# Moving an addition to the stop behind the row of maxima, and a small softmax away from a turn's boundary, in a two-layer cross-attention kernel

## The chip, the core and the metric

One core of one Trainium2 chip runs the whole program. The metric is device time in microseconds (us). The kernel before takes 3610.84 us, the median of three runs (3610.59 to 3620.91). A profiled execution of it took 3614.53 us. Everything is float32.

Five engines work side by side: PE (TensorE, matrix products; its weight loads are listed as PEld), DVE (VectorE), ACT (ScalarE), POOL (GpSimd) and SP (SyncE, which here issues the DMAs). Each takes its own instructions in its own order and waits on semaphores for the others.

## What is computed

Two cross-attention layers follow each other. Layer 0 has two attentions over one context of 1024 tokens: one over 1020 text tokens, one over the last 4 ("ip") tokens, whose scores also depend on the text attention's result (`qsem`).

```python
# layer 0, per batch b (4), head h (20), 512 queries, head size 16
scores_t = einsum('bhsd,bhtd->bhst', q, k_t) * attn_scale
probs_t  = softmax(scores_t)
text_out = einsum('bhst,bhtd->bhsd', probs_t, v_t)
attn_scores = einsum('bhsd,bhnd->bhsn', q, k_ip) * attn_scale
qsem = l2norm(einsum('bhst,bte->bhse', probs_t, text_ehs))     # e = 512
sem  = einsum('bhsn', qsem, l2norm(ip_ehs))
probs_ip = softmax(attn_scores + SEM_SCALE * sem) * spatial_mask
out = (text_out + probs_ip @ v_ip) @ W_out + b_out + x
# layer 1: the same without sem: 77 text tokens, 947 ip tokens
out = (softmax(q k) v + softmax(q k_ip) v_ip) @ Wo.T + bo + out
```

## The kernel before

**Turns, groups, units, stops.** A turn is 128 queries of one batch: 16 turns. A turn has 5 groups of 4 heads, so 80 groups, numbered g in the list `G`. A group has two units of two heads. A unit has four parts (part0 to part3): products of the exponentials with the context and the values, for layer 0. After each part comes a stop, so a group has eight stops, k = 0 to 7 (the first to the eighth), and part0 of the second unit lies between stop k=3 and stop k=4. `stop` (L1019) puts the other work between the parts:

- `item()` (L1013) takes one step from the queues `sub`, `late`, `proj`, the first that isn't empty. `late` holds the end of a turn (below), `proj` the projections of the next batch.
- At k=0 and 1, `fill0(g+1, k)`: the scores of the next group into PSUM (tile sc), copied to SBUF by ACT (L490, tiles e) and reduced to maxima m by DVE.
- At k=2, 4, 5, 6, `l1_step()`: one step of layer 1, four per head group. A step has on PE the products mx for the next head group's maxima and ex for this one's scores. When a head group's last step is done, `do_sub` is put into `sub`: PE transposes the maxima (pt_nm) and DVE adds them to the queries (qa), which the next ex needs.
- At k=2, `max0(g+1)` (L721): PE transposes m (tile mx), DVE reduces it (zz), transposes it (STREAM_TRANSPOSE zt), SP writes zt to DRAM in four pieces (zd, L735) and reads it back to all partitions (bc, L737). Then it puts four functions `do_exp` into the queue `ew`. Each adds bc to one of the group's four tiles e on DVE (L87, e<-e,bc), and ACT takes the exponential (L748).
- `end_stop(k)` (L1007) takes functions out of `ew` and runs them.

The exponentials of group g+1 are needed from part0 of its first and of its second unit on; POOL forms differences and sums of them (L750, L824, L843, L845).

**The end of a turn.** After a turn's last group, `finish(turn)` (L869) runs `norms()` at once and puts six steps into `late`: exps, shares, turn_ip, add_ip, turn_out, multiply. exps is the softmax of the ip scores as far as its exponential: four small DVE operations on `sem` and `pe`, which wait for ACT's `rn`, then one ACT exponential of `pe` (L910). shares divides by the sums, turn_ip transposes the probabilities on PE (pt_p), and multiply calls layer1(turn), which puts x_part, second and start of layer 1 behind them. Layer 1's steps of this turn begin with start.

**What sets the order.** Matmuls, transposes and all that goes through `vec` are kept in program order on PE and DVE (mm, tr and vec, L76 to L92); a scheduler places the rest. Where a helper records the operation, the profile shows its line: L77 for a matmul, L87 for DVE. In the changed kernel lines behind L462 stand one to five lines later.

Of the kernel before, what the change touches and what calls it, by code (L numbers as in the profile page):

```python
# [55 lines left out]
def xattn_pair(ctx_stack: ExitStack, tc: tile.TileContext, a: dict, out: bass.AP):  # L56
# [19 lines left out]
    def mm(out, lhsT, rhs, start, stop, on=False):  # L76
        tc.keep_in_program_order(nc.tensor.matmul(out, lhsT=lhsT, rhs=rhs, start=start, stop=stop, skip_group_check=on))  # L77
# [13 lines left out]
    def tr(out, in_, ident):  # L91
        tc.keep_in_program_order(nc.tensor.transpose(out, in_, ident))  # L92
# [11 lines left out]
    def tp(name):  # L104
        turn_of[0] += 1
        if tail[0]:
            return ps_tp.tile([P, 512], F32, tag="tp", name=name)
        if idle[0] and turn_of[0] % 4:
            return ps_qs.tile([P, 512], F32, tag=f"qs{turn_of[0] % 4 - 1}", name=name)
        return ps_tp.tile([P, 512], F32, tag="tp", name=name)  # L110
# [39 lines left out]
    def load_x(b, s, ns, pl, tag):  # L150
        t = pl.tile([P, ns, C], F32, tag=tag, name=f"{tag}_{b}_{s}")
        nc.sync.dma_start(t, a["x"][b, s * P : (s + ns) * P, :].rearrange("(t p) c -> p t c", p=P))
        return t
# [89 lines left out]
    def zero_below(t):  # L243
        nc.gpsimd.memset(t[64:, NC - 1, :], 0.0)
        return t
# [210 lines left out]
    late = deque()  # L456
# [3 lines left out]
    hold = [0]  # L460
    ready = {}
    pend = []  # L462
    ew = deque()

    def load_quad(l, z, turn, g):
# [214 lines left out]
    def l1_step():  # L680
        if stops[0] < hold[0]:
            return
        if l1:
            l1.popleft()()
        elif pend:
            pend.pop()()
# [182 lines left out]
    def finish(turn):  # L869
        b, s = TURNS[turn]  # L870
        w, z, name = state.pop(turn), zs[b], f"0_{turn}"

        def small(tag, shape):
            return (st2 if tag in ("pT", "oT") else big).tile(shape, F32, tag=tag, name=f"{tag}_{name}")

        def wide(t, n=NIP):
            return t.unsqueeze(2).to_broadcast([P, H, n])

        z.xr[turn] = xr = load_x(b, s, 1, st3, "xr")
        nc.gpsimd.tensor_tensor(xr, xr, bo[0].unsqueeze(1).to_broadcast([P, 1, C]), ALU.add)  # L880
        pv, ss, ips = w["pv"], w["ss"], w["ips"]
        r = small("r", [P, H])
        o = small("o", [P, H, D])
        sem = small("sem", [P, H, NIP])
        n2 = small("n2", [P, H])
        rn = small("rn", [P, H])
        pe = small("pe", [P, H, NIP])
        mx = small("mx", [P, H])
        sums = small("sums", [P, H])
        re = small("re", [P, H])  # L890


        def norms():

            vec.reciprocal(r, pv[:, :, V0W - 1])
            vec.tensor_tensor(n2, ss[:, :, 0], ss[:, :, 1], ALU.add)
            vec.tensor_tensor(n2, n2, r, ALU.mult)
            vec.tensor_tensor(n2, n2, r, ALU.mult)
            vec.tensor_scalar(n2, n2, EPS2, None, ALU.max)
            nc.scalar.activation(rn, n2, AF.Ln)  # L900
            nc.scalar.activation(rn, rn, AF.Exp, scale=-0.5)
            vec.tensor_tensor(o, pv[:, :, 0:D], wide(r, D), ALU.mult)
            vec.tensor_tensor(sem, pv[:, :, D : D + NIP], wide(r), ALU.mult)

        def exps():
            vec.tensor_tensor(sem, sem, wide(rn), ALU.mult)
            vec.scalar_tensor_tensor(pe, sem, SEM_SCALE, ips, ALU.mult, ALU.add)
            vec.tensor_reduce(mx, pe, AX.X, ALU.max)
            vec.tensor_tensor(pe, pe, wide(mx), ALU.subtract)
            nc.scalar.activation(pe, pe, AF.Exp)  # L910

        def shares():
            vec.tensor_reduce(sums, pe, AX.X, ALU.add)
            vec.reciprocal(re, sums)
            vec.tensor_scalar(re, re, spat[:, s : s + 1], None, ALU.mult)
            vec.tensor_tensor(pe, pe, wide(re), ALU.mult)

        of2, box = o.rearrange("p h d -> p (h d)"), {}

        def turn_ip():  # L920
            pt = tp(f"pt_p_{name}")
            tr(pt[: H * NIP, 0:P], pe.rearrange("p h n -> p (h n)"), ident)
            box["pT"] = small("pT", [H * NIP, P])
            vec.tensor_copy(box["pT"], pt[: H * NIP, 0:P])

        def add_ip():
            pt = tp(f"pt_ip_{name}")
            mm(pt[:, 0:C], box["pT"], z.vip, True, True)
            vec.tensor_tensor(of2, pt[:, 0:C], of2, ALU.add)

        def turn_out():
            pt = tp(f"pt_o_{name}")
            for c, (c0, n) in enumerate(CK):
                tr(pt[:n, c * P : (c + 1) * P], of2[:, c0 : c0 + n], ident)
            box["oT"] = zero_below(small("oT", [P, NC, P]))
            vec.tensor_copy(box["oT"][:, 0:2].rearrange("p c s -> p (c s)"), pt[:, 0 : 2 * P])
            vec.tensor_copy(box["oT"][:64, 2, :], pt[:64, 2 * P : 3 * P])

        def multiply():
            pt = tp(f"pt_y_{name}")  # L940
            for c in range(NC):
                mm(pt[:, 0:C], box["oT"][:, c, :], wo0[:, c, :], c == 0, c == NC - 1)
            vec.tensor_tensor(xr[:, 0, :], pt[:, 0:C], xr[:, 0, :], ALU.add)
            layer1(turn)

        norms()
        late.extend([exps, shares, turn_ip, add_ip, turn_out, multiply])


    z, (turns, keys0, last_k, v0, vip, keys1, v1, q0) = projections(0)  # L950
# [55 lines left out]

    def end_stop(k):  # L1007
        stops[0] += 1
        for _ in range({5: 2, 6: 1, 7: 1}.get(k, 0)):
            if ew:  # L1010
                ew.popleft()()

    def item():  # L1013
        for q in (late,) if tail[0] and l1 else (sub, late, proj):
            if q:
                q.popleft()()
                break

    def stop(gi, k):  # L1019

        item()
        if k < 2:
            fill0(gi + 1, k)
        if k in (2, 4, 5) or k == 6 and gi < len(G) - 2 or ending[0] and k < 2:
            l1_step()
        if k == 2:
            max0(gi + 1)
        end_stop(k)
# [9 lines left out]
    for gi, (turn, g) in enumerate(G):  # L1038
        b, s = TURNS[turn]
        n = gi % NQ  # L1040
        ending[0] = gi == len(G) - 1
        if n == 1 and b + 1 < B:
            zs[b + 1], steps = projections(b + 1)
            proj.extend(steps)
        if n == NQ - 2:
            while proj:
                proj.popleft()()
        for i in range(2):
            u = units.pop((gi, i))
            for k, part in enumerate((u.part0, u.part1, u.part2, u.part3)):  # L1050
                part()
                stop(gi, 4 * i + k)
                if k == 2:
                    ahead(gi + i, 1 - i)
            for c in range(2):
                es.pop((gi, i, c))
        if g == HG - 1:
            finish(turn)

    idle[0] = tail[0] = True  # L1060
    while late:
        item()
        if len(l1) > 5:
            l1_step()
        stops[0] += 1
# [28 lines left out]
```

## Time and profile before

| what | value |
|---|---|
| median of three runs | 3610.84 us |
| profiled execution | 3614.53 us |
| its span, first to last instruction | 3612.8 us |
| mean granted PE clock | 0.973 of full speed |
| DVE additions e<-e,bc, 128x1024 | x160, mean 1230 ns |
| DVE additions e<-e,bc, 128x768 | x160, mean 1123 ns |
| ACT exponential of e (L748) | x320, mean 1057 ns |
| DVE idle until DMA bc<-zd | 2.2 us in 2 waits |
| PE sc idle until ACT e L490 | 47.9 us in 31 waits |

The page of a profile gives the busy time of each engine as a share of the span, the chain of work that ended last, and groups of instructions. A timeline line reads: start, duration, engine, source line, operation, tile written <- tiles read, shapes, count; in brackets the engine's idle time before it and what ended it. Durations are us, unless ns is written. "sc", "ex", "mx" and "b" are PSUM tiles; "xs", "xv", "xs_t", "xv_t" the context and its sums and differences; "mx" is used both for the transposed row of maxima of layer 0 (mx<-ident,m) and for layer 1's maxima (mx<-kq,qq).

From about 218 to 3437 us the groups follow each other at a nearly constant pace; before lies the first batch's projection, after it a tail of 175.8 us in which layer 1 of the last turns is finished with a mean granted clock of 0.69.

### The profile page before, as it was taken

The page shows a single profiled execution, that of the slowest core. Times are in us where ns is not written, and L with a number is a line of the kernel's source. Part 1 is how long each engine was busy: PE and PEld are TensorE (multiplying, and loading weights), DVE is VectorE, ACT ScalarE, POOL GpSimd, SP SyncE. Part 2 cuts the span into 40 slices and gives each one's busy share as a digit, 9 for nine tenths or more (in the row PEclk, how much of TensorE's full clock was granted, in tenths as well). Part 3 has the DMA queues.
Part 4 walks back from the last instruction along what each step waited for, and adds up shares of the span by engine and source line. Part 5 has one row for each costly group of instructions (what it writes and reads, how often), then busy time and mean ns, then how long its engine had stood idle before and what let it go on. Part 6 is the DMA issues. An engine that isn't in the chain of part 4 may idle for free.

```text
span 3612.8 us, 74199 instructions
## 1 busy us (share of the span) xinstructions
PE 3496.2 (97%) x29060; PEld 2787.8 (77%) x29060; DVE 2101.1 (58%) x3814; ACT 1471.5 (41%) x2807; POOL 1021.5 (28%) x1050
## 2 busy tenths in 40 slices
PE   7999999999999999999999999999999999999989
PEld 6777777777788777877777788777778777777766
DVE  2344555666655655566664655656666666666644
ACT  1333344444443443444443443444444444444422
POOL 2322222323332222233222232222323323332310
PEclk9999999999999999999999999999999999999976
DMA  6454332222344243222234434222232222222211
GB/s 210 107 130 118 96 67 41 44 42 55 81 98 114 56 103 97 56 52 41 58 78 112 97 83 102 57 60 44 48 84 49 46 45 52 43 47 42 47 31 32
DMA packets 700571, 258.76 MB, mean 72 GB/s; under 512 B 567952, under 2 KB 673904, under 8 KB 700224
## 3 DMA queue, kind: packets, MB, share of 16 engines
q1 hardware_dynamic: 699184, 250.42, 30.9%
q8 instruction: 232, 3.80, 0.5%
q0 software_dynamic: 864, 3.41, 0.4%
q14 instruction: 115, 0.94, 0.1%
q10 hardware_dynamic: 176, 0.20, 0.0%
HBM read 213.51 MB, written 40.33 MB: 70 GB/s over the span
## 4 chain that ended last, share of the span: by engine, by line
PE 85%; DVE 7%; ACT 3%; issue 2%; DMA 1%; SPq 1%; POOL 0%; POOLq 0%; ACTq 0%; DVEq 0%
PE b L77 50%; PE ex L77 6%; PE pv L77 5%; PE mx L77 4%; PE sc L77 4%; PE pt_k L77 4%; PE pt_v L77 4%; DVE e L87 4%; PE pt_y L77 2%; PE pt_q L77 2%; ACT e L490 2%; DVE m L87 1%; PE mx L92 1%; ACT e L748 1%; ACT junk L828 1%
## 5 line engine op out<-in xcount | busy, mean ns | idle before, releaser
L77 PE MATMUL b<-xv_t,e 128*128 128x277 f32 x2560 | 662.3, 401 | 1.7 <-DVE c L87 1.6
L77 PE MATMUL b<-xv,e 128*128 128x277 f32 (+1 forms) x2560 | 649.4, 406 | 2.8 <-ACT e L748 2.8
L77 PEld LDWEIGHTS b<-xv,e 128*128 128x128 f32 x2560 | 478.7, 189 | 134.7 <-ACT e L748 3.4
L77 PEld LDWEIGHTS b<-xv_t,e 128*128 128x128 f32 x2560 | 476.2, 191 | 108.7 <-DVE c L87 4.0
L748 ACT ACTIVATE e<-e 128x1024 f32<-128x1024 f32 x320 | 338.2, 1057 | 462.9 <-DVE e L87 462.8
L843 POOL TENSOR_TENSOR e<-e,s 128x512 f32<-128x512 f32 x160 | 224.0, 1400 | 982.5 <-PE b L77 982.4
L87 DVE TENSOR_REDUCE m<-mx 128x2 f32<-128x870 f32 (+3 forms) x345 | 366.7, 1066 | 115.4 <-PE ex L77 92.2
L87 DVE TENSOR_REDUCE m<-sc 128x256 f32<-128x1024 f32 (+1 forms) x320 | 343.3, 1088 | 135.4 <-PE sc L77 119.1
L551 ACT ACTIVATE e<-ex 128x1024 f32<-128x1024 f32 x320 | 325.7, 1019 | 209.0 <-PE ex L77 208.0
L490 ACT COPY e<-sc 128x1024 f32<-128x1024 f32 x320 | 320.4, 1010 | 177.6 <-PE sc L77 150.5
L77 PE MATMUL mx<-kq,qq 16*128 16x512 f32 x1280 | 380.2, 668 | 6.3 <-DMA qq<-q1d 4.0
L77 PE MATMUL ex<-qa,kq 19*128 19x128 f32 x5120 | 382.2, 291 | 3.8 <-DVE qa L87 3.1
L87 DVE TENSOR_TENSOR e<-e,bc 128x1024 f32<-128x1024 f32 x320 | 369.8, 1177 | 2.2 <-DMA bc<-zd 2.2
L750 POOL TENSOR_TENSOR e<-e 128x512 f32<-128x512 f32 x160 | 205.7, 1285 | 571.2 <-ACT e L748 567.1
L87 DVE TENSOR_TENSOR c<-b,p 128x256 f32<-128x256 f32 x320 | 134.1, 419 | 389.2 <-PE b L77 341.0
L828 ACT ACTIVATE junk<-c 128x256 f32<-128x256 f32 x480 | 198.6, 414 | 395.7 <-DVE c L87 391.2
L77 PEld LDWEIGHTS ex<-qa,kq 19*128 19x128 f32 x5120 | 324.5, 194 | 16.9 <-issue 6.3
L77 PE MATMUL b<-xs,e 128*128 128x256 f32 x1280 | 335.1, 407 | 0.0
L77 PE MATMUL b<-xs_t,e 128*128 128x256 f32 x1280 | 320.0, 393 | 4.3 <-POOL e L843 4.3
L77 PE MATMUL b<-xs_t,s 128*128 128x256 f32 x1280 | 302.7, 379 | 0.0
L77 PEld LDWEIGHTS b<-xs,e 128*128 128x128 f32 x1280 | 240.7, 198 | 48.8 <-issue 2.1
L77 PEld LDWEIGHTS b<-xs_t,e 128*128 128x128 f32 x1280 | 231.5, 190 | 55.4 <-issue 13.9
(190 smaller groups left out, 4173.6 us busy)
## 6 DMA issues: line engine op xcount, KB each, us to landing
kq<-kd SPq DMA_DIRECT2D x640, 64.0 KB
v1q<-v1d SPq DMA_DIRECT2D x80, 373.5 KB
bc<-zd SPq DMA_DIRECT2D x80, 256.0 KB
xv<-v0d SPq DMA_DIRECT2D x480, 42.0 KB
xv_t<-v0d SPq DMA_DIRECT2D x320, 42.0 KB
L_xattn_W_k<-in_L_xattn_W_k_dram SPq DMA_DIRECT2D x13, 640.0 KB
L_xattn_Wv_ip<-in_L_xattn_Wv_ip_dram SPq DMA_DIRECT2D x13, 640.0 KB
raw<-in_ctx_dram SPq DMA_DIRECT2D x32, 256.0 KB
```

Source lines behind the costliest of these rows:

```text
L77: tc.keep_in_program_order(nc.tensor.matmul(out, lhsT=lhsT, rhs=rhs, start=start, stop=stop, skip_group_check=on))
L87: return lambda *args, **kw: keep(getattr(self.engine, name)(*args, **kw))
L92: tc.keep_in_program_order(nc.tensor.transpose(out, in_, ident))
L490: nc.scalar.copy(e[i].rearrange("p h t s -> p (h t s)"), ps[i].rearrange("p h n -> p (h n)"))
L551: nc.scalar.activation(e.rearrange("p i j s -> p (i j s)"), ps.rearrange("p i n -> p (i n)"), AF.Exp)
L748: nc.scalar.activation(flat, flat, AF.Exp)
L750: nc.gpsimd.tensor_tensor(e[:, 1], e[:, 1], e[:, 0], ALU.subtract)
L828: nc.scalar.activation(junk, x, AF.Square, accum_out=self.w["ss"][:, self.h + r, k : k + 1])
L843: nc.gpsimd.tensor_tensor(self.e("11"), self.e("11"), self.s2, ALU.add)
```

## The change

A new queue `after` takes exps out of `late`. It is emptied by one function at the end of the second stop (k=1), behind fill0, and drained before the tail. In `late`, three empty steps stand in exps' place, so that `late` has eight steps in place of six before layer 1's three. And end_stop takes one function from `ew` at each of the stops k=2, 5, 6, 7, in place of two at k=5 and one each at k=6 and k=7. As `stop` calls max0 before end_stop, the function taken at k=2 runs behind max0's.

```diff
@@ xattn_pair @@
     pend = []
+    after = deque()
     ew = deque()
...
@@ finish @@
         norms()
-        late.extend([exps, shares, turn_ip, add_ip, turn_out, multiply])
+        after.append(exps)
+        late.extend([lambda: None] * 3 + [shares, turn_ip, add_ip, turn_out, multiply])
...
@@ end_stop @@
     def end_stop(k):
         stops[0] += 1
-        for _ in range({5: 2, 6: 1, 7: 1}.get(k, 0)):
-            if ew:
-                ew.popleft()()
+        if k in (2, 5, 6, 7) and ew:
+            ew.popleft()()
+        if k == 1 and after:
+            after.popleft()()
...
     idle[0] = tail[0] = True
+    while after:
+        after.popleft()()
     while late:
         item()
```

The functions that are moved, as they stand in both kernels:

```python
def exps():
    vec.tensor_tensor(sem, sem, wide(rn), ALU.mult)
    vec.scalar_tensor_tensor(pe, sem, SEM_SCALE, ips, ALU.mult, ALU.add)
    vec.tensor_reduce(mx, pe, AX.X, ALU.max)
    vec.tensor_tensor(pe, pe, wide(mx), ALU.subtract)
    nc.scalar.activation(pe, pe, AF.Exp)

def do_exp(i, c):
    e, mine = es[gi, i, c], bc[:, 2 * i : 2 * i + 2, :]
    ...
    nc.scalar.activation(flat, flat, AF.Exp)
```

## The prediction

> **What bounds the kernel now.** I read the profile in this order: busy shares, chain of waits, then the timeline of one ordinary group, of one turn's boundary, and of two waits that the change will repeat.
>
> ```profile
> PE 3496.2 (97%) x29060; PEld 2787.8 (77%) x29060; DVE 2101.1 (58%) x3814; ACT 1471.5 (41%) x2807; POOL 1021.5 (28%) x1050
> ...
> PE 85%; DVE 7%; ACT 3%; issue 2%; DMA 1%; SPq 1%; POOL 0%; POOLq 0%; ACTq 0%; DVEq 0%
> ```
>
> TensorE is 97% busy and 85% of the chain that ended last. Anything that keeps it from waiting is worth at most the missing 117 us; anything that makes it wait is paid in full. So each edit is priced by one question: does PE wait longer or shorter?
>
> **The loop and the queue ew.** Group g's third stop calls max0(g+1), which puts four additions into ew. Before the loop ew is drained. Old: stops 6, 7, 8 take 2+1+1, so it is empty when the next four come. New: end_stop takes one at stops 3, 6, 7, 8. At stop 3 it runs after max0, so what it takes is not a leftover but the *first* of the four just put in. The order of instructions of the changed kernel says so too: on DVE the first addition of group g+1 stands directly behind STREAM_TRANSPOSE zt of the same group. It reads bc, whose journey has only just begun. The additions are kept in program order on DVE, so everything behind it waits for that DMA too. An ordinary group before:
>
> ```profile
> 1643.39 0.21 DVE L87 STREAM_TRANSPOSE zt<-zz 128x32 f32<-128x32 f32 x1
> ...
> 1643.76 4.07 PE L77 MATMUL b<-xv,e 128*128 128x298 f32 x16
> ...
> 1645.77 0.35 SPq L737 DMA_DIRECT2D bc<-zd  x1
> ...
> 1657.89 1.22 DVE L87 TENSOR_TENSOR e<-e,bc 128x1024 f32<-128x1024 f32 x1
> ```
>
> See that the addition comes 14.3 us after zt ends (1643.60): the DMA round trip costs nothing there. bc is issued 2.17 us after zt's end, behind the four zd writes that it waits for. How long from bc's issue to an addition that really waits? All 80 groups together waited 2.2 us, in two waits; one of them shows it:
>
> ```profile
> 625.10 0.34 SPq L737 DMA_DIRECT2D bc<-zd  x1
> ...
> 628.63 2.09 DVE L87 TENSOR_TENSOR e<-e,bc 128x1024 f32<-128x1024 f32 x2 [1.66 <-DMA bc<-zd]
> ```
>
> 3.53 us. The other wait (issue 273.2, start 278.31) took 5.1 us among other loads; that is the upper end.
>
> **Edit 1, the first addition at the third stop.** Counted from zt's end. Release: bc issue 2.3 (SP often has one kq load in between), landing and start +3.53, addition +1.23 (mean of its 160), the copy pv behind it +0.2, hand-over to PE 0.15 (qa's end 461.58 to ex 461.73): **7.4 us**. Queued behind it on DVE: pv (frees the PSUM bank of the next t1 product), c, pv, m, nmz, then qa. PE's cover: the 16 matmuls of part 0 end at 4.2, one step of layer 1 adds 1.17 with its start (1648.30 to 1649.47): 5.5; a query product pt_q adds 1.74: 7.2. By the dependences in the changed order, the 79 groups divide so:
> - 28 have part 0 and one step, then need the bank that pv frees: 7.4-5.5 = 1.9 us; 53 us. In 5 of them SP has two window loads ahead of bc that wait for part 0's first product: +0.9 each, 4.5.
> - 15, the second of each turn, need the ip probabilities (turn_ip, now at stop 5) right after part 0. shares' four small operations now follow the addition, 1.1 us (before: 958.93 to 960.02): 8.5-4.2 = 4.3 us; 64.5 us.
> - 14, the third of each turn, have pt_q: 0.2 each, one without the step 1.3: 4.
> - 22 have projection products: 14 nothing, 6 about 0.5, 2 about 1.4: 6.
> Sum **132 us** of PE waiting. From 5.1 us in place of 3.53, release at 9.0, each class by its own cover (102 + 89 + 26 + 20): 237. The other three additions stay covered, and stop 6 has one fewer; I give that nothing.
>
> **What the waits do to the clock.** The granted clock by stretches:
>
> ```profile
> 1188.20:1191.60 3.40, 1.80 (x34) 1.46 (x34) 3.20 (x8) 2.28 (x4) 0.00 (x0) 1.00 0.00 0
> 1191.60:1195.00 3.40, 3.40 (x9) 2.66 (x9) 3.33 (x6) 1.77 (x2) 0.00 (x0) 0.50 0.28 70
> ```
>
> The columns are length, then PE, PEld, DVE, ACT, POOL busy, clock, DMA. A PE gap of 1.60 us (1188.42 to 1190.02) is followed by 3.4 us at 0.50: eight matmuls took 3.57 us there for 1.99, so 1.6 us lost. The Trainium skill (TensorE: Matmul & The Clock Gate, "Why this matters for your kernels") says to leave no gaps over about 3 us; by it the 28 waits of 1.9 us cost no clock and only the 15 of 4.3 do, 15 x 1.6 = 24 us. The row says that 1.6 us can be enough; another of 1.62 us at 1429.3 had no dip. I take three quarters of the 28 and all 15: 34 + 24 = **58 us**. By the skill 24.
>
> **Edit 2, three empty items ahead of shares.** exps leaves `late`, three empties come in: the next turn's start moves from the third stop to the fifth. Layer 1's steps keep their rate (4 per group), but their phase shifts by one step. Before, a group's last step ran at stop 3, and item() at stop 4 did do_sub, so that part 0 (4 us) lay between pt_nm and the ex that needs qa. After, the last step runs at stop 5, do_sub at stop 6, and the ex of the same stop follows. In the changed order 1 of 80 pt_nm has a product between, before 67. Turn 0 before already stands so:
>
> ```profile
> 460.98 0.27 PE L92 MATMUL pt_nm<-ident,nmz 128*128 128x128 f32 x1
> 461.19 1.13 PE L77 MATMUL mx<-kq,qq 16*128 16x512 f32 x4
> 461.73 1.16 PE L77 MATMUL ex<-qa,kq 19*128 19x128 f32 x16
> 462.82 2.17 PE L77 MATMUL pv<-e,v1q 128*32 128x128 f32 x72
> ```
>
> From pt_nm to the next work 1.84 us; covered, pt_nm takes 0.11 and the step 1.10 in the chain. 0.63 us x 66 = **42 us** (none if DVE were early, which it can't be: qa needs pt_nm). q1's stores and loads move with it, behind bc instead of ahead of zd in the third groups: no cost that I see, bc gains there. One layer-1 step more (10 instead of 9) is left for the tail: 175.8 us there for 29 steps and more; less its place in the loop, **+3 us**.
>
> **Edit 3, exps behind stop 2's maxima.**
>
> ```profile
> 956.26 0.27 ACT L910 ACTIVATE pe<-pe 128x80 f32<-128x80 f32 x1 [1.96 <-DVE pe L87]
> 956.43 2.02 ACT L490 COPY e<-sc 128x1024 f32<-128x1024 f32 x2
> ...
> 958.51 1.67 PE sc L77 x32
> ```
>
> (The last line is the chain of waits, the others the timeline.) At a turn's boundary ACT's exponential of pe waits for four small DVE operations of 0.2 to 1.2 us; the two score copies queue behind it, and PE's next sc waits 3.16 us. Twelve turns' boundaries show such a gap (10 of about 3.16, two of 1.6: 35 us of the 47.9 us that the view of waits gives for PE sc behind ACT e). With exps behind fill0 the copies no longer queue there, but they need about 2 us after the square at 954.31, so about 1 us stays: 2.1 x 12 = 25 us back, and part of the dips that followed, 10 us: **-35 us**. Ends: nothing, and all of it, 35 + 12 x 1.6 = -54. The moved operations then lie in front of c, m and zz at the third stop, where PE has 2 us of products to cover them.
>
> **Sum.** 132 + 58 + 42 + 3 - 35 = +200 us. The profiled execution took 3614.5 us (span 3612.8), so 3814.5; the runs' median is 3610.84, 3.7 lower, so **3811 us**.
>
> **Rivals.**
> *Slower round trip.* If every waiting addition sees the 5.1 us of the loaded sample: waits 237, dips at about 57 groups 91, phase 42, tail 3, boundary -25: 3959 us. For it: kq loads of 64 KB now stand between zd and bc. Against: clean groups reissue quickly, and most of the trace has DMA at 2 to 4 tenths. Chance 0.15.
> *Nothing waits.* If the addition found bc landed, as the words of the change say (a fourth addition left over), only -35 + 42 + 3 would remain: 3621 us, no change. Against: ew is empty each time max0 fills it. Chance 0.02.
> *Faster: the boundary decides.* If in addition the ex did not wait for qa, the boundary's whole 54 us would come back, less the tail's 3: 3560 us. It decides only where the bc wait is under about 0.5 us of PE per group. For it: the gap of 3.16 us is real and regular. Against: 7.4 us of release stands against 4.2 to 5.5 of cover. Chance 0.03.
> The forecast has 0.80.
>
> **Numbers.** Low end of my case: waits 1.4 and 3.8 where I have 1.9 and 4.3 (101), clock by the skill (24), phase 42, boundary -54, tail 3: +116, 3727. The high end takes in a good part of the slower round trip: 3920. The range 3727 to 3920 leaves about 0.2 out. A change of under 0.3% (11 us) can't be told from none. Faster 0.03, same 0.02, slower 0.95.
>
> **What would show it.** "DMA bc<-zd" becomes DVE's cause of about 80 waits of 3 to 5 us; PE sits idle before b<-xs_t behind DVE pv, and before pt_p behind DVE pe; dips of the clock once or so per group rather than one per turn; pt_nm followed within 0.8 us by ex; the sc gap at the boundary near 1 us. If DVE's first addition starts later than zt by 6 us without PE idling, edit 1 is wrong; if the clock stays at 0.97, the skill's rule was the better one.

## The result, and the profile after

| | before | after |
|---|---|---|
| median of four runs each, us | 3610.72 | 3971.13 |
| range of the runs, us | 3610.58 to 3620.91 | 3954.91 to 3977.86 |
| profiled execution, us | 3614.53 | 3954.91 |
| mean granted PE clock | 0.973 | 0.949 |
| PE idle until something releases it, gaps over 0.25 us, in sum | 112 us | 318 us |
| half clock between the rows of groups 1 and 79 (zt to zt) | 68 us | 311 us |

The changed kernel is slower by a ratio of 1.0984 (95% interval 1.0945 to 1.1023), 360 us between the medians and 340 us between the profiled executions. The forecast was 3811 us, with a range of 3727 to 3920: the direction is right, the size is not, and the result lies outside the range. The last two rows of the table are sums over the trace, of PE's gaps and of the stretches in which its clock is granted at 0.50. Eight 128x256 products that took 1.99 us in an undisturbed place took 3.55 us at a clock of 0.50 (2851.94 us below), so a stretch of half clock is counted as half lost: 243 us more of it cost about 121 us. With 205 us more of gaps this gives 326 of the 340.

The page of the kernel after: busy shares, chain of waits, and the group of additions.

```profile
PE 3627.6 (92%) x29060; PEld 2873.0 (73%) x29060; DVE 2139.1 (54%) x3815; ACT 1468.6 (37%) x2807; POOL 1043.1 (26%) x1050
...
PE 66%; DVE 13%; DMA 10%; issue 4%; SPq 3%; ACT 2%; POOL 2%; DVEq 0%; ACTq 0%; POOLq 0%
...
L87 DVE TENSOR_TENSOR e<-e,bc 128x1024 f32<-128x1024 f32 x320 | 406.5, 1271 | 520.1 <-DMA bc<-zd 520.1
```

PE has fallen from 97% to 92% busy and from 85% to 66% of the chain; DVE and DMA hold 23% of it, where they held 8%. The additions now wait 520.1 us for bc, where they waited 2.2: 79 waits of 6.6 us in the mean, longer than the 3 to 5 us that the prediction looked for, since DVE is idle from zt's end on. An ordinary group after (the timeline, PE, DVE and SP lines):

```profile
2844.59 0.21 DVE L87 STREAM_TRANSPOSE zt<-zz 128x32 f32<-128x32 f32 x1
...
2847.10 0.35 SPq L738 DMA_DIRECT2D bc<-zd  x1
...
2850.48 1.22 DVE L87 TENSOR_TENSOR e<-e,bc 128x1024 f32<-128x1024 f32 x1 [5.68 <-DMA bc<-zd]
2851.62 0.17 DVE L87 COPY pv<-b 128x21 f32<-128x21 f32 x1
...
2851.94 3.55 PE L77 MATMUL b<-xs_t,e 128*128 128x256 f32 x8 [1.96 <-DVE pv L87]
```

bc is issued 2.30 us after zt's end, the addition starts 3.38 us later, pv follows at once, and PE restarts 7.14 us after zt's end: the forecast's chain, which said 7.4, with 1.96 us of waiting where it said 1.9. (That the wait fits so closely is in part luck: PE's cover was also 0.3 us shorter than forecast, 5.2 in place of 5.5.) PE's waits of the kernel after show which terms of the sum came out so and which did not (columns: total us, number, longest).

```profile
PE b L77 <- DVE pv L87: 73.3, 31, 4.3
PE pt_p L92 <- DVE pe L87: 67.0, 15, 5.2
PE b L77 <- POOL e L844: 36.2, 30, 1.8
PE mx L77 <- DMA qq<-q1d: 23.4, 10, 3.7
PE pt_v L77 <- DMA L_xattn_W_v<-in_L_xattn_W_v_dram: 19.2, 4, 7.0
...
PE sc L77 <- ACT e L491: 9.9, 13, 2.8
```

The first two lines are edit 1 as it was argued. The last is the boundary's gap, 47.9 us before and 9.9 now. Lines three to five were in no sum: the POOL sum of part 0 (4.3 us before), layer 1's query loads (4.0) and a weight load (7.7).

### The profile page after: what moved, and what is told of

Its sections match the earlier page's. It is cut to its first block, busy times and chain, and to the rows that moved or that the text cites. A ratio compares the mean times of both kernels' runs of the same rounds, so it can differ in the third digit from the quotient of the medians.

```text
span 3953.2 us, 74078 instructions
## 1 busy us (share of the span) xinstructions
PE 3627.6 (92%) x29060; PEld 2873.0 (73%) x29060; DVE 2139.1 (54%) x3815; ACT 1468.6 (37%) x2807; POOL 1043.1 (26%) x1050
## 3 DMA queue, kind: packets, MB, share of 16 engines
q0 software_dynamic: 864, 3.41, 0.3%
## 4 chain that ended last, share of the span: by engine, by line
PE 66%; DVE 13%; DMA 10%; issue 4%; SPq 3%; ACT 2%; POOL 2%; DVEq 0%; ACTq 0%; POOLq 0%
PE b L77 38%; DMA bc<-zd 6%; PE pv L77 5%; PE ex L77 4%; DVE m L87 4%; PE sc L77 4%; PE mx L77 4%; PE pt_k L77 4%; PE pt_v L77 3%; DVE e L87 3%; DVE den L87 2%; PE pt_y L77 2%; DMA zd<-zt 2%; PE pt_q L77 1%; SPq L736 1%
## 5 line engine op out<-in xcount | busy, mean ns | idle before, releaser
L87 DVE TENSOR_TENSOR e<-e,bc 128x1024 f32<-128x1024 f32 x320 | 406.5, 1271 | 520.1 <-DMA bc<-zd 520.1
L77 PE MATMUL b<-xs_t,e 128*128 128x256 f32 x1280 | 385.0, 453 | 109.6 <-DVE pv L87 73.3
L844 POOL TENSOR_TENSOR e<-e,s 128x512 f32<-128x512 f32 x160 | 248.7, 1554 | 760.9 <-PE b L77 760.8
L77 PE MATMUL mx<-kq,qq 16*128 16x512 f32 x1280 | 389.9, 680 | 28.8 <-DMA qq<-q1d 23.4
L825 POOL TENSOR_TENSOR s<-e,e 128x512 f32<-128x512 f32 x160 | 203.6, 1273 | 765.0 <-ACT e L749 732.3
L77 PEld LDWEIGHTS b<-xs_t,e 128*128 128x128 f32 x1280 | 271.4, 223 | 177.1 <-issue 85.5
L77 PEld LDWEIGHTS ex<-qa,kq 19*128 19x128 f32 x5120 | 326.8, 195 | 26.1 <-DVE qa L87 10.4
L77 PE MATMUL b<-xs_t,s 128*128 128x256 f32 x1280 | 321.9, 397 | 0.0
L751 POOL TENSOR_TENSOR e<-e 128x512 f32<-128x512 f32 x160 | 204.9, 1281 | 441.9 <-ACT e L749 441.4
L77 PE MATMUL b<-xs,e 128*128 128x256 f32 x1280 | 320.9, 394 | 0.0
L77 PEld LDWEIGHTS b<-xs_t,s 128*128 128x128 f32 x1280 | 262.4, 205 | 43.0 <-ACT p L843 0.2
```

The source lines that it names most:

```text
L87: return lambda *args, **kw: keep(getattr(self.engine, name)(*args, **kw))
L751: nc.gpsimd.tensor_tensor(e[:, 1], e[:, 1], e[:, 0], ALU.subtract)
L825: nc.gpsimd.tensor_tensor(self.s2, self.e("21"), self.e("22"), ALU.add)
L844: nc.gpsimd.tensor_tensor(self.e("11"), self.e("11"), self.s2, ALU.add)
```

## The experiments

Ratios are against the kernel before on the same chip, in three rounds; in brackets their 95% intervals. The median of before was 3615.94 us for "The empty steps filled" and for the second run under "The wait taken away". It was 3617.89 for the first run there and for "One stop later", "The third addition earlier" and "A version faster than both", and 3617.42 for the other four.

**Edit 1 alone, and edits 2 and 3 alone.** The first takes only end_stop's new line, the second all the rest.

```diff
-        for _ in range({5: 2, 6: 1, 7: 1}.get(k, 0)):
-            if ew:
-                ew.popleft()()
+        if k in (2, 5, 6, 7) and ew:
+            ew.popleft()()
```

> Edit 1 alone: the kernel before with the additions taken at stops 3, 6, 7, 8; late and exps are untouched. Main theory (the first addition's wait for bc is nearly the whole loss): turn_ip stays at the third stop ahead of the row of maxima, so the 15 second groups wait 2 us and not 4.3; some 43 groups at 2 us, 22 projection groups at 3 us, and half clock behind most of them: +150 of waiting and +90 of clock, 3830 to 3880 us; DVE e<-e,bc waits about 500 us on DMA bc<-zd, and no PE gap of 1.4 us behind the POOL sum L843 e<-e,s. Rival (the shifted phase of layer 1 makes half of the loss): 3710 to 3760 us here, with the rest in the run of edits 2 and 3.

Measured: **4100.36 us, 1.1348 (1.1318 to 1.1377)**, that is +483 us: more than the whole change, and outside both theories. PE's waits of this run:

```profile
PE ex L77 <- DVE qa L87: 102.2, 42, 5.3
...
PE pt_ip L77 <- DVE qa L87: 42.6, 13, 3.7
PE pt_k L77 <- DVE qa L87: 38.6, 8, 5.2
PE pt_cT L92 <- DVE qa L87: 33.1, 8, 5.6
```

and one of its groups, first in the timeline, then by stretches (length, then busy us of PE, PEld, DVE, ACT and POOL, clock, DMA share, GB/s):

```profile
2934.63 0.27 PE L92 MATMUL pt_nm<-ident,nmz 128*128 128x128 f32 x1
...
2940.30 1.23 DVE L87 TENSOR_TENSOR e<-e,bc 128x1024 f32<-128x1024 f32 x1 [5.72 <-DMA bc<-zd]
2941.45 0.17 DVE L87 COPY pv<-b 128x21 f32<-128x21 f32 x1
2941.53 0.28 DVE L87 TENSOR_TENSOR qa<-pt_nm,qq 128x128 f32<-128x128 f32 x1
...
2941.96 2.08 PE L77 MATMUL ex<-qa,kq 19*128 19x128 f32 x16 [2.10 <-DVE qa L87]
2943.97 4.07 PE L77 MATMUL pv<-e,v1q 128*32 128x128 f32 x72
```

```profile
2941.40:2944.80 3.40, 2.84 (x32) 2.59 (x36) 2.03 (x7) 2.18 (x4) 1.26 (x1) 0.55 0.04 10
2944.80:2948.20 3.40, 3.40 (x65) 2.80 (x56) 0.00 (x0) 0.40 (x2) 0.00 (x0) 0.50 0.04 10
```

In the old phase (start at its place before the change) do_sub stands one stop behind the row of maxima. So qa, which feeds the next ex and also frees the PSUM bank of the projection that comes next (pt_k, pt_cT), is queued on DVE behind the addition that waits. 78 of the 79 groups show a gap of PE within 17 us behind the row (zt's end); over groups 1 to 78 these gaps sum to 262 us. And the wait of 2.10 us costs more than itself: behind it, with ex first, the clock stays at half for two stretches of 3.41 us and not one. Over groups 1 to 78 half clock is 509 us against 68 before. With the empty steps of edit 2, which move do_sub to a later stop, the same wait costs 285 us and not 483 (below).

> Edits 2 and 3 alone: exps behind the second stop and three empty steps, the additions as in the kernel before. Main theory: boundary -50, exposed qa +42, PE waiting for the POOL sum in some 25 groups 1.4 us each, +35, tail +3, some clock: 3610 to 3670 us, and the wait on bc stays at 2 us. Rival (the shifted phase makes half of the loss): 3760 to 3800 us. If the 1.4 us gaps behind the POOL sum are absent here and in edit 1 alone, they need both.

Measured: **3691.96 us, 1.0212 (1.0183 to 1.024)**, +75 us: 22 us above the main theory's range, 68 below the rival's. The forecast had +10 for these two edits. Its PE waits:

```profile
PE b L77 <- POOL e L844: 36.4, 30, 1.8
PE pt_v L77 <- DMA L_xattn_W_v<-in_L_xattn_W_v_dram: 24.8, 5, 6.9
PE mx L77 <- DMA kq<-kd: 13.3, 3, 4.7
PE sc L77 <- ACT e L491: 7.3, 9, 2.8
```

The first two lines stand in the kernel after too (36.2 and 19.2 us). In the next run, which keeps the old phase and has one empty step less, they are at 4.3 and 7.2 us, and the third has no line of 2 us or more: so they come with the shifted phase or the third empty step. One of the 30 gaps (timeline):

```profile
3036.47 1.75 DVE L87 RECIPROCAL den<-den 128x256 f32<-128x256 f32 x1
...
3039.28 1.43 DVE L87 TENSOR_TENSOR e<-e,bc 128x1024 f32<-128x1024 f32 x1
3040.74 1.06 ACT L749 ACTIVATE e<-e 128x1024 f32<-128x1024 f32 x1 [2.81 <-DVE e L87]
...
3041.87 1.27 POOL L751 TENSOR_TENSOR e<-e 128x512 f32<-128x512 f32 x1 [2.25 <-ACT e L749]
...
3042.29 1.67 DVE L87 TENSOR_TENSOR e<-e,bc 128x768 f32<-128x768 f32 x1
...
3043.10 1.98 POOL L844 TENSOR_TENSOR e<-e,s 128x512 f32<-128x512 f32 x1
3043.88 1.48 DVE L87 SCALAR_TENSOR_TENSOR e<-e,drop,bc 128x256 f32<-128x256 f32 x1
3045.13 1.99 PE L77 MATMUL b<-xs_t,e 128*128 128x256 f32 x8 [1.37 <-POOL e L844]
```

Layer 1's reciprocal and maxima now come at the seventh stop, ahead of the third addition. The addition, its exponential and POOL's difference (L751) slip behind them, and POOL, in order, gets late to the sum (L844) that PE's next products need.

**The boundary's gain without the phase.** Edits 2 and 3, but with two empty steps, and the last two steps of layer 1's beginning in one, so that start stays at its stop.

```diff
-        late.extend([lambda: None] * 3 + [shares, turn_ip, add_ip, turn_out, multiply])
+        late.extend([lambda: None] * 2 + [shares, turn_ip, add_ip, turn_out, multiply])
...
-        late.extend([x_part, second, start])
+        late.extend([x_part, lambda: (second(), start())])
```

> exps behind the second stop, but with two empty steps, and second and start joined in one step, so that start stays at its stop and 67 of 80 pt_nm keep a product between them and ex; the additions as in the kernel before. Main theory: only the boundary's gain is left, -35 to -55: 3556 to 3576 us, PE sc idle behind ACT e about 12 us. Rival (the time of the boundary is lost again at the next stop, behind exps in DVE's queue): 3605 to 3615 us. The difference to edits 2 and 3 alone is the price of the phase: 45 us by the prediction's terms, 80 or more if the gaps behind the POOL sum belong to it.

Measured: **3579.18 us, 0.9907 (0.988 to 0.9933)**, -38 us, 3 us above the main theory's range. Its waits:

```profile
PE sc L77 <- ACT e L491: 21.8, 30, 0.8
PE pt_nm L92 <- DVE ips L87: 13.6, 14, 1.1
PE pt_v L77 <- DMA L_xattn_W_v<-in_L_xattn_W_v_dram: 7.2, 3, 5.0
...
PE b L77 <- POOL e L844: 4.3, 6, 1.4
```

The forecast's -35 for the boundary is confirmed, and the phase, with the third empty step, costs 3691.96 - 3579.18 = 113 us. A little of the boundary's gain comes back as a wait of the next group: 14 times about 1 us of pt_nm behind DVE's copy of ips, while sc's wait falls from 47.9 to 21.8 us and not to the expected 12.

**An addition that is really left over.** The prediction's second rival quotes a description of the change as a fourth addition left over from the group before; the changed kernel has none. This run does: it is the run before with one addition left to the next group's third stop, where it is taken in max0, ahead of bc's read.

```diff
@@ max0 @@
+        if not idle[0] and ew:
+            ew.popleft()()
         bc = big.tile([P, 4, P], F32, tag="bc0", name=f"bc{name}")
@@ end_stop @@
-        for _ in range({5: 2, 6: 1, 7: 1}.get(k, 0)):
-            if ew:
-                ew.popleft()()
+        if (k in (5, 6, 7) or ending[0]) and ew:
+            ew.popleft()()
```

> What the title says: one addition is left in the queue at each group's end and taken in the next group's third stop behind the row's transposes and its writes, ahead of the bc read; the others at stops 6, 7, 8; exps and phase as in the run with two empty steps. Main theory: no addition waits for its own bc, so no loss by it; but the last exponential comes one stop before the sum s2 of the second unit needs it, so PE has 6 us of products against about 6.5 us of addition, exponential and two POOL sums: 0.5 us in 79 groups, 3600 us (3565 to 3650). Rival (the later place frees stops 6 to 8, and this pays): below 3556 us. Rival (the sum is much later): over 3700 us.

Measured: **3608.38 us, 0.9975 (0.9966 to 0.9984)**: 8 us above the main theory's 3600, and 29 above the run that it builds on. DVE waits 2.8 us for bc in all, so there is no journey in it. New among PE's waits are 12.1 us behind the POOL sum L846 and 11.8 us behind ACT's copy p, at the beginning of a unit; the later exponential that was expected to push them back is the likely cause, but was not moved by itself. All gaps over 0.25 us sum to 113 us against 98, so about half of the 29 us lies in no such gap, and was not followed further.

**The wait taken away.** The order of the changed kernel, with another operand in the first addition.

```diff
-            if c == 0:
+            if (i, c) == (0, 0) and gi:
+                vec.tensor_tensor(e, e, ident.unsqueeze(1).unsqueeze(1).to_broadcast([P, 2, TH, P]), ALU.add)
+            elif c == 0:
```

> The changed kernel in the same order of instructions, but from the second group on the first addition of each group adds the identity tile, which lies in SBUF from the start, instead of bc: it leaves out the subtraction of the maximum there, and with it the wait for bc. Main theory (the wait is what edit 1 costs, not the addition's place on DVE): the 285 us between edits 2 and 3 alone and the changed kernel go nearly all, 3685 to 3710 us, PE gaps behind DVE pv and pe near nothing. Rival (the addition's 1.23 us ahead of pv, qa and shares is a good part): 3750 to 3850 us.

Measured: **3684.65 us, 1.0185 (1.0164 to 1.0207)**, the time of edits 2 and 3 alone (1.0212) within their intervals, and at the lower edge of the main theory. The addition follows zt at once:

```profile
2654.20 0.21 DVE L87 STREAM_TRANSPOSE zt<-zz 128x32 f32<-128x32 f32 x1
2654.33 1.18 DVE L87 TENSOR_TENSOR e<-e,ident 128x1024 f32<-128x1024 f32 x1
2655.43 0.17 DVE L87 COPY pv<-b 128x21 f32<-128x21 f32 x1
```

So the place of the addition costs nothing that these runs can tell; its wait costs 1.0984 against 1.0185, some 285 us. The same edit in edit 1 alone tells whether that holds in the old phase too:

> Edit 1 alone, with the identity tile in bc's place in the first addition of each group from the second on: it leaves out the subtraction of the maximum there, and with it the wait. Main theory (edit 1 alone costs 483 us because qa, which layer 1's next product needs at once in the unshifted phase, stands behind the addition that waits): 3610 to 3635 us. Rival (in the unshifted phase the addition's own place ahead of qa costs too): 3680 us or more.

Measured: **3611.72 us, 0.9985 (0.9973 to 0.9997)**, the time of the kernel before. All 483 us of edit 1 alone are the wait.

**One stop later.** `k in (3, 5, 6, 7)` in the changed kernel.

> The changed kernel with the first addition one stop later, at the fourth in place of the third: pv, which frees a PSUM bank, now stands ahead of it on DVE; the journey of bc is as long as before. Main theory (what is queued behind the waiting addition decides, not that it waits): DVE still waits for bc about 300 us or more, but PE's gaps behind pv go; qa and c remain behind it: 3690 to 3740 us. Rival (any addition that waits costs alike): 3900 us or more.

Measured: **3757.28 us, 1.0388 (1.0366 to 1.041)**. DVE still waits 381.4 us for bc, in 77 waits, three quarters of the 520.1; yet of the 285 us only about 70 are left. Its longest line of PE's waits is now

```profile
PE pt_nm L92 <- DVE nmz L87: 52.4, 55, 3.1
```

The copy pv and shares' work on pe stand ahead of the addition here, and neither shows among PE's longer waits; of what is behind the addition, nmz is what PE waits for. What a wait costs is decided by what is queued behind it. The run is some 20 us above the main theory's range: the nmz line is what that theory did not count.

**The third addition earlier.** Edits 2 and 3 alone with the additions `{4: 1, 5: 2, 7: 1}`.

> Edits 2 and 3 alone, with the additions at stops 5, 6, 6 and 8 in place of 6, 6, 7 and 8: the third one, whose POOL difference stands ahead of the POOL sum that the next group's first products need, comes a stop earlier. Main theory (with the shifted phase that difference comes too late behind layer 1's reciprocal and maxima on DVE): the 30 gaps of PE b behind POOL e L844 (36 us, and dips behind some) go: 3692 less 40 to 50, 3640 to 3655 us. Rival (the gap belongs to POOL's own speed beside DVE): it stays, 3685 to 3700 us.

Measured: **3629.01 us, 1.0031 (1.002 to 1.0043)**. The line of PE b behind POOL L844 is gone from the waits, and 63 us with it, more than the gaps and dips that were counted. Of the 51 us between the two profiled executions, 27 are fewer gaps over 0.25 us and 17 are half of 34 us less half clock. So DVE's order makes the gap. POOL's speed is not ruled out as a part of it: the same order puts POOL's sum beside DVE's fourth addition, where it took 1.98 us, and in this run it no longer runs there (last section).

**The empty steps filled.** Edits 2 and 3 alone, with two of the three empty steps replaced by

```diff
+        def fill_in():
+            if proj:
+                proj.popleft()()
```

> Edits 2 and 3 alone, where two of the three empty steps take a step of the projections when there is one. Main theory (the empty steps used up stops that the projections had, so these come later and in denser order, and PE waits for the weights of pt_v, 25 us against 8): that wait and its dips go, 3692 less 20 to 40, 3650 to 3672 us; the gaps of 1.37 us stay. Rival (the weights come late because SP's queue has q1's transfers elsewhere): 3685 us or more.

Measured: **3665.03 us, 1.0145 (1.0123 to 1.0166)**, 27 us less than edits 2 and 3 alone. PE's wait for the weights of pt_v falls from 24.8 to 11.3 us, the POOL gaps stay (40.4 us in 36), as does layer 1's wait for its keys (15.1 us). An "empty" step is not free: the queues share one step per stop, so each can take a stop from the projections.

**A version faster than both.** The boundary's gain, the old phase, and the additions one stop earlier than before, `{4: 2, 5: 1, 6: 1}`.

> The run with two empty steps and joined second and start, with the additions one stop earlier: two at the fifth stop, one each at the sixth and seventh. bc has landed by then in most groups (6 us after the row against about 9). If the 0.74 us gap of PE sc at the second stop comes from the last exponential lying ahead of the score copies on ACT, it goes: 3579 less 24 and a little clock, 3545 to 3560 us. Rival (at the fifth stop bc is still late in the loaded groups, and DVE holds back c and qa there): 3590 to 3640 us.

Measured: **3553.3 us, 0.983 (0.9807 to 0.9853)**, faster than the kernel before by 1.7%, and by the two ratios (0.983 against 1.0984) about 10.5% faster than the changed one. Its busy shares, and its waits for bc and of sc:

```profile
PE 3479.3 (98%) x29060; PEld 2771.4 (78%) x29060; DVE 2045.3 (57%) x3814; ACT 1478.7 (41%) x2807; POOL 998.0 (28%) x1050
```

```profile
DVE e L87 <- DMA bc<-zd: 48.4, 43, 4.7
...
PE sc L77 <- ACT e L491: 8.3, 10, 1.0
```

DVE waits 43 times for bc, 48.4 us in all, and PE's gaps within 17 us of the row sum to 12.6 us against 9.3 before: here the wait fills time that DVE had. The 0.74 us gaps of sc at the second stop are gone (47.9 us before, 21.8 with the boundary mended, 8.3 here), as was expected if ACT has the last exponential behind it when the scores come.

## Why the prediction was right in kind and wrong in size

| term | forecast, us | measured |
|---|---|---|
| edit 1, waits of PE | 132 | 181: gaps within 17 us of the row, 222.6 in the kernel after less 41.8 in edits 2 and 3 alone |
| edit 1, half clock | 58 | 101: half of (310.6 - 109.2) us of half clock in groups 1 to 78 |
| edits 2 and 3 | +10 (42 + 3 - 35) | +75 |
| sum | +200 | +360 |

**Edit 1: mechanism right, two terms too small.** That the first addition is taken, not a leftover one, that pv and pe are behind it, and that PE restarts some 7.4 us after zt's end are as forecast. By the prediction's classes, with the gaps of the same groups in edits 2 and 3 alone taken off:

| class | forecast, us | after, less edits 2 and 3 alone |
|---|---|---|
| 28 groups that need pv's bank | 57.5 | 69.5 - 13.3 = 56 |
| 15, the second of each turn | 64.5 | 67.0 - 0.8 = 66 |
| 14, the third of each turn | 4 | 24 |
| 22 with projection products | 6 | 62 - 28 = 34 |

The first two are right. Wrong were the lines "14, the third of each turn, have pt_q: 0.2 each" and "22 have projection products: 14 nothing, 6 about 0.5, 2 about 1.4". In the third groups nine gaps (19.6 us) end with layer 1's query load qq, which had not landed, and four (3.7 us) with pt_nm: the step that was counted as PE's cover was itself late. In the projection groups SP issued bc as late as 6.2 us after zt's end, mostly behind other loads, where the forecast took 2.3 for all, and in 17 of the 22 the addition began 7 to 10.4 us after zt's end, not 5.8.

**Half clock: 101 where 58 stood.** The term took one dip of 3.4 us for each wait of the class of 15 and for three quarters of the class of 28, and none elsewhere. In 13 of the 15 groups that wait for pt_p the half clock is 6.8 us or more, two stretches, and the third and the projection groups, which had no dips in the sum, have them. In the class of 28, 7 groups have no half clock and 16 have one stretch. What failed is the carrying over of one row, a gap with dense products behind it, to gaps with other products behind them.

**Edits 2 and 3: the loss lay beside what was priced.** The boundary's -35 is confirmed by -38. The exposed qa is there: in edits 2 and 3 alone pt_nm, mx, ex, pv stand 1.84 us apart from first to last start in 61 cases, the figure used. Between two runs with almost no other gap, the third addition earlier (191.97 us for an ordinary turn) and the fastest version (190.4), with their remaining gaps taken off (0.63 and 1.77), it is 2.7 us per turn or 0.54 per group where 0.63 was taken; this is an estimate, as the two runs differ in more than the phase. What failed is that the sum put everything else that moves with the step at nothing: the empty steps' use of stops (27 us by filling them), POOL's sum behind the third addition (63 us by moving that), and the loads, "no cost that I see" (13.3 us of waiting for layer 1's keys in edits 2 and 3 alone; what delays them was not tested). I followed do_sub to its new stop and priced what it read; I did not ask what the other half of the step, layer 1's reciprocal and maxima on DVE, now stood in front of.

**The rivals.** The slower round trip gave 3959 us, 12 from the median, but by luck and not by its cause: the median addition starts 5.98 us after zt's end, against 5.83 in the forecast and 7.4 in the rival, and most of the class of 28 wait 1.9 to 2.4 us. Late loads as it has them are found in the projection groups alone, and in a few others. Its size came from the terms above. "The boundary decides" was right that the boundary's gain is real, -38 us; beside the wait for bc it decides nothing.

**The rule and the row.** Gaps of 2 us were followed by half clock, as the row at 1188.4 us had it: in the kernel after,

```profile
2848.75:2852.16 3.41, 1.45 (x22) 1.23 (x22) 1.68 (x5) 1.45 (x2) 1.26 (x1) 1.00 0.77 133
2852.16:2855.57 3.41, 3.41 (x9) 2.71 (x9) 2.00 (x4) 1.03 (x3) 1.26 (x1) 0.50 0.02 5
```

PE was idle 1.96 us and busy 1.45 of the 3.41, and the next 3.41 us ran at 0.50, with eight products taking 3.55 us. The advice of the Trainium skill (TensorE: Matmul & The Clock Gate, "Why this matters for your kernels"), no gaps over about 3 us, gave 24 us in the prediction where 101 were measured; the measurement decides against it here.

**What stays open.** The parts of the phase do not add up to 113 us one by one (63, 27 and some 36 for qa make 126), so they overlap; the overlap was not measured. The traces divide it another way: of the 105 us between the profiled executions of edits 2 and 3 alone and of the run with the old phase, 34 are gaps over 0.25 us and 41 are half of 82 us of half clock. The other 30 lie in no such gap, where the exposed qa would be. Layer 1's key loads that come late (13 us in edits 2 and 3 alone) were seen in the trace and not moved.

## What to carry to other kernels

Price a wait by what is queued behind it in order on its engine and by PE's cover at that place: the same journey of bc cost 483, 285 and about 70 us, by what stood behind the addition, and in the fastest version hardly anything that PE's gaps show. A step that is delayed by empty steps moves every instruction in it, and takes turns from whoever shares the queue: check each engine's order for what the moved step now stands in front of, not only for what it now waits for. And before an operation is pulled ahead to fill a stop, compare its distance to the load that it reads: here, two stops behind the row (the addition began 7.7 us after zt's end in the median) was free, one stop behind cost about 70 us, and directly behind cost 285.

## What the runs showed of the hardware

Short idling was often enough to halve PE's clock, and not always. After 1.96 us of idling the next stretch ran at 0.50 (2852.16 us in the kernel after); 7 groups of the class of 28, with gaps of 1.9 to 2.7 us, show no half clock.

How long a dip lasted went with the products behind the gap. Sums over the trace of edit 1 alone, groups 1 to 78: where layer 1's ex (19 rows) filled the largest part of a dip's first 3.41 us, all 28 dips lasted two stretches or more, also the eight in which PE was busy for 3.3 us or more of the first. Where pv (32 columns) filled it, 16 of 17 dips lasted one. In the kernel after, 25 of the 33 dips with b first (128 rows and columns) lasted one. Why was not tested.

In edit 1 alone there were 258 us more of gaps near the row than before (262 against 4), and with them 440 us more of half clock, worth about 220. So a microsecond of waiting cost close to two.

DVE and POOL held each other up in some pairs of instructions. In the gap shown for edits 2 and 3 alone, DVE's two parts of the fourth addition took 1.67 and 1.48 us, and POOL's sum of 128x512 (L844) 1.98; POOL's difference L751, beside the first part, kept its 1.27. In the run with the third addition earlier the parts were done before the sum began:

```profile
3002.16 0.96 DVE L87 TENSOR_TENSOR e<-e,bc 128x768 f32<-128x768 f32 x1
3003.05 0.47 DVE L87 SCALAR_TENSOR_TENSOR e<-e,drop,bc 128x256 f32<-128x256 f32 x1
...
3003.56 1.27 POOL L844 TENSOR_TENSOR e<-e,s 128x512 f32<-128x512 f32 x1 [1.25 <-PE b L77]
```

The 0.7 us by which the sum is longer are half of the gap of 1.37. It was no single case: over edits 2 and 3 alone, 60 of the 68 sums that overlap the second part took about 2.0 us, and 247 of the other 252 took 1.3.
